# Deformable convolutions and a mixture of experts on one core: another order of the pixels in a tile's partitions

## The chip, the cores and the metric

The kernel runs on one core of a Trainium2 chip. The metric is the device time of one launch in microseconds. The core has five instruction streams that run beside each other and meet at semaphores: PE (matrix products and transposes), DVE (vector work), ACT (activations, scaled copies), POOL (here it only issues indirect DMAs) and SP (issues the plain DMAs). Sixteen DMA engines move the data of both issuers.

## The reference, cut to what matters

The input x has 4 images of 256 channels and 64 x 64 pixels. After a normalisation over channels, three modulated deformable 3 x 3 convolutions follow, each with a ReLU, then a residual sum, a layer norm over channels, and a mixture of 8 experts (the best two for each pixel).

```python
def _deform_layer(x, w_off, b_off, w, b):
    om = conv3x3(x, w_off) + b_off                 # 27 channels
    off = om[:, :2 * K].reshape(B, K, 2, H, W)     # K = 9 taps
    mask = jax.nn.sigmoid(om[:, 2 * K:])
    ys = gy + base_y + off[:, :, 0]
    xs = gx + base_x + off[:, :, 1]
    sampled = _bilinear(x, ys, xs) * mask[:, None] # [B, C, K, H, W]
    return einsum('bikhw,oik->bohw', sampled, wk) + b

for wo, bo, w, b in params:                        # three layers
    x = relu(_deform_layer(x, wo, bo, w, b))
```

For every pixel and tap, four neighbouring pixels with all their 256 channels are blended, at a place that depends on the data.

## The kernel before, in words

An image is cut into 8 blocks (NB) of 512 pixels (BLK, 8 image rows), and a block into 4 tiles (TPB) of 128 pixels, two image rows each. In a tile, partition p holds pixel p % 64 of row p // 64. The twelve pairs of layer and image are run as stages in the order of `self.stages` (L860): (0,0), (1,0), (0,1), (2,0), (1,1), (0,2), (2,1), (1,2), (0,3), (2,2), (1,3), (2,3), with the layer first. For each block of a stage `main_block` runs; beside it, in small steps (`step`, `aside`), the preparation of the next layer's blocks, and from a queue with credits (`pump`) the experts' work of images that are through.

The source of the samples is a table in DRAM for each image and layer (`store_table`): one row of 2048 bytes per pixel, with its 256 channels and their differences to the image row below. Two table rows that follow each other are two pixels side by side, so 4096 bytes hold all that one bilinear sample needs.

The plan of a block is made in `off_block`. PE computes the offset convolution into the PSUM tile `po`, in four strips of 32 partitions; ACT copies it with the bias to `om` [128, 512], pixels along the free axis in raster order (L337). Then for each tile t a matmul with `om[:, t*128:(t+1)*128]` as its stationary operand turns it (L342), so that pixel t*128+p arrives in partition p of `pm`. DVE adds `base` (the host's table of each partition's pixel coordinates, L921 to L925), takes floors and fractions, and stores the indices `idx` and the coefficients `cf`.

`main_block` runs over the 9 taps k and the 4 tiles. For each pair POOL issues one indirect DMA (L452) that fetches for each of the 128 partitions the 4096 bytes at the table row in `idx`, into one of 10 buffers `g`. DVE blends in one direction (L458), ACT scales the left half (L463), DVE adds the right half (L468), giving `s` with pixels in partitions; PE transposes it (L472) and ACT copies the result to `sT` (L477), channels in partitions and pixels along the free axis. PE multiplies `sT` with the tap's weights into `acc` (L480), which holds both halves of the output channels for the 512 pixels in one PSUM buffer, across all taps.

At the end of a block `acc` is evicted: ACT takes the first half of the channels (L500), DVE the second (L501), both with bias and ReLU. For layers 0 and 1 the target is the window `w` of the next layer (10 rows of 66 pixels with a border), for layer 2 it is the tile `r` for the tokens. What follows (`rows_done`, `store_table`, `off_block`, or `tokens`) reads pixels in raster order.

The order of the program is that of the loops and generators. The order in which instructions stand on an engine is made from it at compile time; the timeline shows L458 and L468 in other orders than the loop's.

Of the kernel before, what the change touches and what calls it, by code (L numbers as in the profile page):

```python
# [10 lines left out]
AF = mybir.ActivationFunctionType  # L11
ALU = mybir.AluOpType
# [9 lines left out]
CC = C // P  # L22
# [4 lines left out]
NB = H * W // BLK  # L27
RPB = BLK // W
J = TPB * K

# [52 lines left out]
class Weave:  # L85
# [231 lines left out]
    def off_block(self, l, b, n, w):  # L317

        nc = self.nc
        nm = f"{l}_{b}_{n}"  # L320


        po = self.ps1.tile([P, BLK], F32, tag="po", name=f"po_{nm}")
        terms = [(k, c) for k in range(K) for c in range(CC)]
        for m, (k, c) in enumerate(terms):
            ky, kx = divmod(k, 3)
            g = m % NQ
            nc.tensor.matmul(  # L328
                po[g * Q : (g + 1) * Q, :],
                lhsT=self.wo[l][:, k, c, :],  # L330
                rhs=w[:, c, ky : ky + RPB, kx : kx + W],
                start=(m < NQ),
                stop=(m + NQ >= len(terms)),
                tile_position=(0, g * Q),
            )
        om = self.small.tile([P, BLK], F32, tag="om", name=f"om_{nm}")
        nc.scalar.activation(om, po, AF.Identity, bias=self.bo[l])  # L337
        yield
        pm = self.ps.tile([P, TPB, 3 * K], F32, tag="tp", name=f"pm_{nm}")
        for t in range(TPB):  # L340

            nc.tensor.matmul(  # L342
                pm[:, t, :],
                lhsT=om[:, t * P : (t + 1) * P],
                rhs=self.strips[:, : 3 * K],
                start=True,
                stop=True,
            )

        def small(tag, shape=(P, 2, J), dt=F32):  # L350
            return self.small.tile(list(shape), dt, tag=tag, name=f"{tag}_{nm}")

        idx = self.plan.tile([P, J], I32, tag="idx", name=f"idx_{nm}")
        cf = self.plan.tile([P, J, 3], F32, tag="cf", name=f"cf_{nm}")
        self.plans[l, b, n] = (idx, cf)

        th = small("th", (P, J))
        nc.scalar.activation(
            th.rearrange("p (t k) -> p t k", k=K), pm[:, :, 2 * K :], AF.Tanh, scale=0.5
        )  # L360
        pos = small("pos")
        for d in range(2):
            nc.vector.tensor_tensor(
                pos[:, d, :].rearrange("p (t k) -> p t k", k=K),
                pm[:, :, d : 2 * K : 2],
                self.base[:, n, d, :, :],
                ALU.add,
            )

        nc.vector.tensor_scalar(pos, pos, -1.0, float(H), ALU.max, ALU.min)  # L370
        pi = small("pi", dt=I32)
        nc.vector.tensor_copy(pi, pos)
        yield
        pf = small("pf")
        nc.vector.tensor_copy(pf, pi)
        up = small("up")
        nc.vector.tensor_tensor(up, pf, pos, ALU.is_gt)
        fl = small("fl")
        nc.vector.tensor_tensor(fl, pf, up, ALU.subtract)
        fr = small("fr")  # L380
        nc.vector.tensor_tensor(fr, pos, fl, ALU.subtract)
        ixf = small("ixf", (P, J))
        nc.vector.scalar_tensor_tensor(
            ixf, fl[:, 0, :], float(TC), fl[:, 1, :], ALU.mult, ALU.add
        )
        nc.vector.tensor_scalar(idx, ixf, float(TC + 1), None, ALU.add)
        yield

        nc.vector.tensor_copy(cf[:, :, 0], fr[:, 0, :])
        for q, (s0, s1) in enumerate(((-0.5, 0.5), (0.5, 0.0))):  # L390
            hf = small(f"hf{q}", (P, J))
            nc.vector.tensor_scalar(hf, fr[:, 1, :], s0, s1, ALU.mult, ALU.add)
            nc.vector.scalar_tensor_tensor(cf[:, :, 1 + q], th, 1.0, hf, ALU.add, ALU.mult)
# [43 lines left out]
    def main_block(self, i, n, wins):  # L437
        nc = self.nc
        l, b = self.stages[i]
        nm = f"{i}_{n}"  # L440
        idx, cf = self.plans.pop((l, b, n))
        tb = self.table(l, b)
        acc = self.ps1.tile([P, CC, BLK], F32, tag="acc", name=f"acc_{nm}")
        for k in range(K):
            sT = self.smT.tile([P, CC, BLK], F32, tag="sT", name=f"sT_{nm}_{k}")
            for t0 in range(0, TPB, 2):
                tp = self.ps.tile([P, CC, 2 * P], F32, tag="tp", name=f"tp_{nm}_{k}_{t0}")
                gs, ss = [], []
                for t in (t0, t0 + 1):
                    j = t * K + k  # L450
                    g = self.gat.tile([P, 2, 2, C], F32, tag="g", name=f"g_{nm}_{j}")
                    nc.gpsimd.indirect_dma_start(  # L452
                        out=g.rearrange("p x s f -> p (x s f)"),
                        out_offset=None,
                        in_=tb,
                        in_offset=bass.IndirectOffsetOnAxis(ap=idx[:, j : j + 1], axis=0),
                    )
                    nc.vector.scalar_tensor_tensor(  # L458
                        g[:, :, 0, :], g[:, :, 1, :], cf[:, j, 0:1], g[:, :, 0, :],
                        ALU.mult, ALU.add,  # L460
                    )
                    s = self.smp.tile([P, C], F32, tag="s", name=f"s_{nm}_{j}")
                    nc.scalar.activation(s, g[:, 0, 0, :], AF.Copy, scale=cf[:, j, 1:2])  # L463
                    gs.append(g)
                    ss.append(s)
                for u in range(2):
                    j = (t0 + u) * K + k
                    nc.vector.scalar_tensor_tensor(  # L468
                        ss[u], gs[u][:, 1, 0, :], cf[:, j, 2:3], ss[u], ALU.mult, ALU.add
                    )  # L470
                    for c in range(CC):
                        nc.tensor.transpose(  # L472
                            tp[:, c, u * P : (u + 1) * P],
                            ss[u][:, c * P : (c + 1) * P],
                            self.ident,
                        )
                nc.scalar.copy(sT[:, :, t0 * P : (t0 + 2) * P], tp)  # L477
            for o in range(CC):
                for c in range(CC):
                    nc.tensor.matmul(  # L480
                        acc[:, o, :],
                        lhsT=self.wk[k][:, c, o * P : (o + 1) * P],
                        rhs=sT[:, c, :],
                        start=(k == 0 and c == 0),
                        stop=(k == K - 1 and c == CC - 1),
                    )
            if n == NB - 1 and i + 1 < len(self.stages):
                self.load_tap(self.stages[i + 1][0], k, i + 1)
            self.step(k)
            self.pump()  # L490
        bk = self.bk[l]
        if l < NL - 1:
            w = wins[n] = self.window(n, nm, False)
            dst = [w[:, o, 1 : RPB + 1, 1 : W + 1] for o in range(CC)]
            src = [acc[:, o, :].rearrange("p (r w) -> p r w", w=W) for o in range(CC)]
        else:
            r = self.big.tile([P, CC, BLK], F32, tag="a", name=f"r_{nm}")
            dst = [r[:, o, :] for o in range(CC)]
            src = [acc[:, o, :] for o in range(CC)]
        nc.scalar.activation(dst[0], src[0], AF.Relu, bias=bk[:, 0:1])  # L500
        nc.vector.tensor_scalar(dst[1], src[1], bk[:, 1:2], 0.0, ALU.add, ALU.max)  # L501
        if l < NL - 1:
            self.rows_done(l + 1, b, n, wins)
        else:
            self.aside(5, self.tokens(b, n, r))
# [432 lines left out]
```

## Time and profile before

Eleven runs give a median of 8170.06 us, from 8149.62 to 8199.07. The profiled execution took 8176.97 us, and its span from the first to the last instruction is 8175.3 us.

| engine | busy, us | share | instructions |
|---|---|---|---|
| PE | 6704.9 | 82% | 27032 |
| DVE | 4918.7 | 60% | 10768 |
| ACT | 3566.5 | 44% | 7368 |
| POOL | 4476.3 | 55% | 4133 |

The granted TensorE clock is 0.926 on average. The DMA engines moved 2314 MB in 744,472 packets, 283 GB/s over the span. The costliest groups by line:

| line, engine | what | count | busy, us | mean, ns |
|---|---|---|---|---|
| L452 POOL | issue of a gather | 3456 | 3766.6 | 1090 |
| L480 PE | product with the tap's weights | 6912 | 3409.1 | 638 |
| L458 DVE | first blend, 128 x 512 | 3456 | 2528.3 | 744 |
| L463 ACT | scaling, 128 x 256 | 3456 | 1673.6 | 511 |
| L468 DVE | second blend, 128 x 256 | 3456 | 1617.3 | 481 |

In a line of the waits, the engine and line on the left stood idle until the one on the right was done; the numbers are the total in us, how often, and the longest. In a line of the timeline stand the start in us, the duration in us, the engine, the line, the operation, and in brackets the idle time before it with what ended it. In a line for one source line stand the shortest, the median and the longest duration in ns. Busy times of engines overlap, so they don't add up to the span.

### The profile page before, as it was taken

Reading aid. Unit: us, or ns where it says so; the run is one execution under the profiler, and the core shown is the slowest. Engines: PE = TensorE matmul, PEld = TensorE weight load, DVE = VectorE, ACT = ScalarE, POOL = GpSimd, SP = SyncE. Lnnn points to the kernel's source line nnn. Section 1 sums busy time; section 2 is a strip of 40 time slices with the busy share of each in tenths; the row PEclk is TensorE's granted clock in tenths of the full one; section 3 lists DMA queues with packets and bytes.
Section 4 is the critical chain, followed back from the end, with each engine's and each line's share of the span. In section 5 each row is a group of like instructions: output and inputs, shape, how many; then the busy total and the mean of one; then the engine's idle time right before and its main releaser. Section 6 shows DMA issues by size and latency. Waiting matters only on the chain. (4 is left out here: it accounts for less than half of the span.)

```text
span 8175.3 us, 91172 instructions
## 1 busy us (share of the span) xinstructions
PE 6704.9 (82%) x27032; PEld 3751.3 (46%) x27032; DVE 4918.7 (60%) x10768; ACT 3566.5 (44%) x7368; POOL 4476.3 (55%) x4133
## 2 busy tenths in 40 slices
PE   5898888888876999998866799998866889896395
PEld 2444444444442555555433455555532455563274
DVE  4776677777774666667665566666754555565201
ACT  3454444445442444545443444545433443443121
POOL 0554666665556566655566565665666544456413
PEclk8999999999997999999988999999978999997697
DMA  5987899998887898988787889898887777787433
GB/s 172 365 305 269 320 324 321 328 329 312 290 289 242 313 326 320 324 318 297 255 302 258 284 312 333 325 332 316 290 286 250 265 271 262 283 286 257 151 124 119
DMA packets 744472, 2314.47 MB, mean 283 GB/s; under 512 B 104344, under 2 KB 148376, under 8 KB 735784
## 3 DMA queue, kind: packets, MB, share of 16 engines
q0 software_dynamic: 544704, 1954.99, 67.2%
q1 hardware_dynamic: 199272, 353.64, 12.2%
q8 instruction: 217, 3.56, 0.2%
q14 instruction: 279, 2.29, 0.1%
HBM read 2167.35 MB, written 249.61 MB: 296 GB/s over the span
## 5 line engine op out<-in xcount | busy, mean ns | idle before, releaser
L452 POOL DMA_INDIRECT g<-tab,idx x3456 | 3766.6, 1090 | 2687.8 <-DVE s L468 1305.9
L480 PE MATMUL acc<-sT,wk 128*128 128x512 f32 x6912 | 3409.1, 638 | 356.6 <-ACT sT L477 232.7
L458 DVE SCALAR_TENSOR_TENSOR g<-g,cf 128x512 f32<-128x512 f32 x3456 | 2528.3, 744 | 478.9 <-DMA g<-tab,idx 383.6
L468 DVE SCALAR_TENSOR_TENSOR s<-g,cf,s 128x256 f32<-128x256 f32 x3456 | 1617.3, 481 | 1601.4 <-ACT s L463 1260.5
L463 ACT ACTIVATE s<-g,cf 128x256 f32<-128x256 f32 x3456 | 1673.6, 511 | 1674.6 <-DVE g L458 1107.8
L480 PEld LDWEIGHTS acc<-sT,wk 128*128 128x128 f32 x6912 | 1332.1, 202 | 2049.4 <-issue 1521.5
L472 PE MATMUL tp<-ident,s 128*128 128x128 f32 x6912 | 1082.0, 283 | 462.0 <-DVE s L468 327.0
L477 ACT COPY sT<-tp 128x512 f32<-128x512 f32 x1728 | 970.7, 587 | 1011.3 <-PE tp L472 688.3
L472 PEld LDWEIGHTS tp<-ident,s 128*128 128x128 f32 x6912 | 823.5, 145 | 947.4 <-issue 499.8
L765 PE MATMUL py<-w,hT 128*128 128x256 f32 x2496 | 637.3, 392 | 69.2 <-ACT hT L760 50.0
L750 PE MATMUL ph<-fzT,w 128*128 128x256 f32 x2496 | 620.0, 392 | 22.0 <-issue 7.8
L750 PEld LDWEIGHTS ph<-fzT,w 128*128 128x128 f32 x2496 | 479.8, 195 | 168.5 <-issue 55.2
L765 PEld LDWEIGHTS py<-w,hT 128*128 128x128 f32 x2496 | 458.5, 192 | 210.1 <-ACT hT L760 107.3
L706 POOL DMA_INDIRECT w<-in_W,wrow x156 | 177.2, 1136 | 653.4 <-issue 307.5
L760 ACT ACTIVATE hT<-ph,w 128x256 f32<-128x256 f32 x624 | 261.3, 470 | 533.4 <-PE ph L750 345.0
L328 PE MATMUL po<-win,wo 128*32 128x512 f32 x2304 | 455.9, 616 | 46.5 <-ACT win L263 35.0
L773 DVE TENSOR_TENSOR y<-py,w 128x512 f32<-128x512 f32 x156 | 107.5, 689 | 461.1 <-PE py L765 457.1
L794 POOL DMA_INDIRECT gy<-ys,slots x256 | 264.2, 1032 | 211.1 <-DVE ta L802 88.7
L681 POOL DMA_INDIRECT zs<-zl,slots x256 | 267.1, 1043 | 136.1 <-issue 70.7
L298 ACT COPY hv<-tpv 128x512 f32<-128x512 f32 x384 | 214.4, 595 | 227.1 <-PE tpv L293 117.0
L328 PE MATMUL po<-win_pre,wo 128*32 128x512 f32 x1152 | 229.7, 644 | 22.7 <-ACT win_pre L422 7.6
L293 PE MATMUL tpv<-ident,vv 128*128 128x128 f32 x768 | 156.8, 285 | 26.4 <-ACT sT L477 17.1
(144 smaller groups left out, 3237.3 us busy)
## 6 DMA issues: line engine op xcount, KB each, us to landing
tab<-hv SPq DMA_DIRECT2D x384, 256.0 KB
g<-tab,idx POOLq DMA_INDIRECT x3456
zt<-zs SPq DMA_DIRECT2D x156, 256.0 KB
ys<-y SPq DMA_DIRECT2D x156, 256.0 KB
wk<-in_conv_w SPq DMA_DIRECT2D x108, 256.0 KB
zs<-nil SPq DMA_DIRECT2D x38, 512.0 KB
xc_pre<-in_x SPq DMA_DIRECT2D x32, 512.0 KB
xr_tok<-in_x SPq DMA_DIRECT2D x32, 512.0 KB
```

Of the source, the lines that this page charges most:

```text
L328: nc.tensor.matmul(po[g * Q : (g + 1) * Q, :], lhsT=self.wo[l][:, k, c, :], rhs=w[:, c, ky : ky + RPB, kx : kx + W], start=(m < NQ), stop= ...
L452: nc.gpsimd.indirect_dma_start(out=g.rearrange("p x s f -> p (x s f)"), out_offset=None, in_=tb, in_offset=bass.IndirectOffsetOnAxis(ap=id ...
L458: nc.vector.scalar_tensor_tensor(g[:, :, 0, :], g[:, :, 1, :], cf[:, j, 0:1], g[:, :, 0, :], ALU.mult, ALU.add,)
L463: nc.scalar.activation(s, g[:, 0, 0, :], AF.Copy, scale=cf[:, j, 1:2])
L468: nc.vector.scalar_tensor_tensor(ss[u], gs[u][:, 1, 0, :], cf[:, j, 2:3], ss[u], ALU.mult, ALU.add)
L472: nc.tensor.transpose(tp[:, c, u * P : (u + 1) * P], ss[u][:, c * P : (c + 1) * P], self.ident,)
L477: nc.scalar.copy(sT[:, :, t0 * P : (t0 + 2) * P], tp)
L480: nc.tensor.matmul(acc[:, o, :], lhsT=self.wk[k][:, c, o * P : (o + 1) * P], rhs=sT[:, c, :], start=(k == 0 and c == 0), stop=(k == K - 1 ...
L681: ins = self.nc.gpsimd.indirect_dma_start(out=self.zs[grp.i % 2], out_offset=bass.IndirectOffsetOnAxis(ap=grp.slots[:, i, m : m + 1], axis=0),
L750: nc.tensor.matmul(ph[:, h, :], lhsT=w1[:, o : o + P], rhs=zT[:, c, :], start=(c == 0), stop=(c == CC - 1),)
L765: nc.tensor.matmul(py[:, u, :], lhsT=hT[h // 2][:, h % 2, u * P : (u + 1) * P], rhs=w2[:, h * C : (h + 1) * C], start=(h == 0), stop=(h == ...
L794: nc.gpsimd.indirect_dma_start(out=g, out_offset=None, in_=self.ys[grp.i % 2], in_offset=bass.IndirectOffsetOnAxis(ap=grp.slots[:, i, m : ...
```

## The change

The order of the 64 pixels of an image row in the 64 partitions of a half tile is changed. Each half row of 32 pixels was laid into 32 partitions in raster order. Now partition 4e + j of such a group holds pixel 8j + e, with e from 0 to 7 and j from 0 to 3. Partitions that lie four apart hold neighbouring pixels; partitions side by side hold pixels that lie 8 apart.

The permutation enters where ACT copies `po` to `om` (the written address jumps by 4 elements for neighbouring pixels), and the host's `base` names the new coordinates. Indices, coefficients, gathers, blends, transposes and products follow in the new order with no other change. It is undone at the eviction: `acc` is read in its own order and written to raster positions, so neighbouring elements are written 8 elements (32 bytes) apart. The pattern has too many dimensions for one instruction, so each of the two becomes one per half row (h).

```diff
-        nc.scalar.activation(om, po, AF.Identity, bias=self.bo[l])
+        nc.scalar.activation(
+            om.rearrange("p (q e j) -> p q j e", e=8, j=4),
+            po.rearrange("p (q j e) -> p q j e", e=8, j=4),
+            AF.Identity,
+            bias=self.bo[l],
+        )
...
             w = wins[n] = self.window(n, nm, False)
-            dst = [w[:, o, 1 : RPB + 1, 1 : W + 1] for o in range(CC)]
-            src = [acc[:, o, :].rearrange("p (r w) -> p r w", w=W) for o in range(CC)]
+            dst = w[:, :, 1 : RPB + 1, 1 : W + 1]
         else:
             r = self.big.tile([P, CC, BLK], F32, tag="a", name=f"r_{nm}")
-            dst = [r[:, o, :] for o in range(CC)]
-            src = [acc[:, o, :] for o in range(CC)]
-        nc.scalar.activation(dst[0], src[0], AF.Relu, bias=bk[:, 0:1])
-        nc.vector.tensor_scalar(dst[1], src[1], bk[:, 1:2], 0.0, ALU.add, ALU.max)
+            dst = r.rearrange("p c (r w) -> p c r w", w=W)
+        dst = dst.rearrange("p c r (h j e) -> p c h r e j", j=4, e=8)
+        src = acc.rearrange("p c (r h e j) -> p c h r e j", h=2, e=8, j=4)
+        for h in range(2):
+            nc.scalar.activation(dst[:, 0, h], src[:, 0, h], AF.Relu, bias=bk[:, 0:1])
+            nc.vector.tensor_scalar(
+                dst[:, 1, h], src[:, 1, h], bk[:, 1:2], 0.0, ALU.add, ALU.max
+            )
...
-    base[:, :, 1] = p % W + k % 3 - 1 + 0 * (n + t)
+    base[:, :, 1] = p // 32 % 2 * 32 + p % 4 * 8 + p % 32 // 4 + k % 3 - 1 + 0 * (n + t)
```

## The prediction

> **What bounds the kernel now.** I read the page's head first, then the groups of instructions by cost, the waits by total, a stretch of the timeline in the steady part, and last the rows of the lines that the diff touches. The page's chain of waits covers only the last part, where the FFN of the fourth image runs alone (PE with 2% is its largest share), so it says nothing of the stages in which the gathers run; those are read from the waits.
>
> ```profile
> DMA  5987899998887898988787889898887777787433
> q0 software_dynamic: 544704, 1954.99, 67.2%
> q1 hardware_dynamic: 199272, 353.64, 12.2%
> ```
>
> The 16 DMA engines are busy 8 to 9 tenths where the convolutions run, and most of that is q0, which carries the gathers. That looks like a DMA bound. The waits say that it is not:
>
> ```profile
> POOL g L452 <- DVE s L468: 1305.9, 1100, 10.4
> DVE s L468 <- ACT s L463: 1260.5, 1220, 20.1
> ACT s L463 <- DVE g L458: 1107.8, 1048, 12.0
> DVE g L458 <- DMA g<-tab,idx: 383.6, 284, 11.6
> ```
>
> The instruction that consumes a gather, L458, waited for the gather's landing 284 times out of 3456, 383.6 us in all. The issuer waits more than three times as long for a free buffer. The timeline shows why:
>
> ```profile
> 1004.11 0.75 DVE L458 SCALAR_TENSOR_TENSOR g<-g,cf 128x512 f32<-128x512 f32 x1
> ...
> 1004.47 1.20 POOL L452 DMA_INDIRECT g<-tab,idx  x1 [1.08 <-DVE s L468]
> ...
> 1004.90 0.51 ACT L463 ACTIVATE s<-g,cf 128x256 f32<-128x256 f32 x1 [1.22 <-DVE g L458]
> ...
> 1005.44 0.48 DVE L468 SCALAR_TENSOR_TENSOR s<-g,cf,s 128x256 f32<-128x256 f32 x1 [0.58 <-ACT s L463]
> ...
> 1005.84 0.74 DVE L458 SCALAR_TENSOR_TENSOR g<-g,cf 128x512 f32<-128x512 f32 x1
> ...
> 1006.19 1.20 POOL L452 DMA_INDIRECT g<-tab,idx  x1 [0.52 <-DVE s L468]
> ```
>
> One sample tile costs 0.75 + 0.51 + 0.48 us in series over DVE, ACT, DVE, and the next L458 starts 1.73 us after the first without waiting for data. Setting the packets of q0 in order of issue against the starts of L458, I find a median of 8.4 us between the moment when a gather's 128 packets are through and its use; 79% have over 4 us, 11% under 1.5 us. Those late ones lie in stages (2,0), (2,1), (1,3) and (2,3), where the next indices come late and POOL issues just in time. So faster fetching can pay only in about 300 gathers, while slower fetching pays nothing until the slack is used up.
>
> **The change, part by part.**
>
> *Order of the rows in a gather.* Nothing is added on POOL or in bytes. What it can alter is how long packets take. The packet records of q0 have 458,752 packets of 4096 bytes with a median of 159 ns and a mean of 183 ns: 82% stand at the floor, 7.9% take over 200 ns and bear nearly all of the excess. An engine moves 8 packets per gather, so stalled ones (about 10 of 128) make the slowest of the 16 engines some 0.9 us late (8 x 24 ns mean, plus two or three hits of some 300 ns on the unluckiest). No run here has the new order, so I bound: all stalls gone, 300 late gathers x 0.9 us = -270 us; excess doubled, two hits more on the unluckiest, 300 x 0.6 = +180 us, and the densest stages (DMA share 0.91) reach 0.91 + 8 x 24 ns / 1.74 us = 1.02, which on (1,0) and (0,1), 1000 us, adds 20 more: +200 us. The nearest row is the spread between stages: offsets differ much by layer (their standard deviation, from the reference's inputs, is 0.48, 0.15 and 0.08 pixels), yet the share of stalled packets moves only between 5.8% and 9.5%. So I let it move by one point of eight, downward because more common rows are read at a time: 270 / 8 = 34, taken as **-30 us**.
>
> *The eviction of acc.* One ACT and one DVE instruction of 512 elements become two each of 256, 96 times.
>
> ```profile
> L500 ACT ACTIVATE win<-acc,bk x64: 670/689/692, 267.9 to 6874.2; 128x512 f32<-128x512 f32 x64
> L501 DVE TENSOR_SCALAR win<-acc,bk x64: 739/752/754, 268.6 to 6874.9; 128x512 f32<-128x512 f32 x64
>   PE acc L480: 148.5, 73
>   DVE win L501: 64.4, 29
>   ACT r L500: 32.4, 12
> L651 DVE TENSOR_REDUCE sf<-r x8: 568/586/594, 2433.0 to 7645.6; 128x32 f32<-128x256 f32 x8
> L662 DVE TENSOR_REDUCE ex<-r x4: 465/466/477, 2431.8 to 7643.1; 128x39 f32<-128x312 f32 x4
> ```
>
> DVE starts 0.7 us after ACT, at ACT's end, though they read and write different halves. I take it that the four new instructions are chained likewise, ACT, DVE, ACT, DVE. Of 256 elements from PSUM, L760 on ACT takes 468 ns and L68 on DVE 536, so some 500 each: 4 x 0.50 + 3 x 0.034 = 2.10 us against 0.69 + 0.034 + 0.75 = 1.47, **+0.63 us**. The elements are now written 32 bytes apart. The one row like it is L651, which reads 256 elements 128 bytes apart in 586 ns; L662 reads 312 in a row in 466, so 256 would take about 408, and the stride costs 178 ns. Below, 0; above, 4 x 0.178 = 0.71 us: the eviction grows by 0.63 to 1.35 us, taken 0.9, nearer the lower end because a read is not a write. If the halves were not chained, 2 x 0.5 = 1.0 us would stand against 1.47, a gain of 0.45 us: the bound below. What waits: ACT's second half waits for DVE, and behind it in ACT's queue stand the copies L477 and the scalings L463 of the next block, behind those PE's matmuls. How often this counts: in 73 of 96 blocks ACT stood idle for the last matmul of acc, in 41 (29 + 12) DVE stood idle for ACT. Between 0.43 and 0.76 I take 0.6: 96 x 0.9 x 0.6 = **+52 us**, bounds 96 x 0.45 x 0.6 = -26 and 96 x 1.35 x 0.76 = +98.
>
> *The copy om (L337).* Still one instruction, 687 ns, written 16 bytes apart: 0 to 2 x 178 = 356 ns, x 96 = 0 to 34 us. PE waited for it in 52 of 96 blocks; half of half: **+10 us**.
>
> *base* is only other numbers in the same 288 KB load: nothing.
>
> Against the Trainium skill, for those who have it: SBUF — State Buffer (section Door 1: The DMA port swizzle) says that each access in a new line of 16 bytes pays. L651 agrees for reads (586 against about 408 ns); no row shows a write. By that rule both stores pay fully, and the sum would be 8177 + 78 + 34 - 30 = 8259 instead of the 8209 below. DMA: Bandwidth & Descriptors (section The descriptor swizzle) gives each engine four partitions in a row, so that the engines now fetch pixels four apart, 8 KB, at a time, and then neighbours. With that map and the sample positions, stalls in the present records are fewer in gathers where more engines read near the same row at once; drawn out to the new order, an estimate with a wide error, about half would go: 8177 + 62 - 135 = 8104.
>
> **Sum.** Against the profiled execution, 8176.97 us (span 8175.3 and 1.7 around it): 8177 - 30 + 52 + 10 = 8209. The median of the eleven runs is 7 us lower, so 8202, said as **8205 us**.
>
> **The rivals.**
>
> *Faster: the fetch gains more than the eviction costs.* Neighbours at a time halve the stalls: 300 x 0.45 = -135, and the eviction has no stride cost, 96 x 0.63 x 0.6 = +36: 8170 - 99 = about 8070 us. It decides from the point where the fetch gives back 62 us, a quarter of 270: stalled packets falling from 7.9% to under 6%. For it: the 24 ns of excess stand mostly in stretches with gathers alone, so gathers disturb gathers. Against it: 8.4 us of slack, and only 284 waits.
>
> *Much slower: the fetch becomes the bound.* If engines that read the same rows queue behind one another and the excess triples (72 ns, 231 per packet), the share of the dense stages (1,0), (0,1), (0,2), (0,3), 2170 us, becomes 0.91 + 8 x 48 / 1740 = 1.13: +280 us, late gathers 300 x 1.2 = +360, the two stores +62: about 8870; doubled only, 8170 + 200 + 62 = 8432. For it: DMA at 0.9. Against it: the spread by layer is small.
>
> *It does nothing for fetching and the eviction is hidden,* for ACT is busy 44% and DVE 60%: 8170. Against it: 41 blocks in which DVE waited for ACT.
>
> Below all of these lies the order in which the instructions stand on each engine: in the trace L458 and L468 alternate singly in some blocks and in pairs in others, so that order is not the loop's, and it can shift when instructions are added. I have no price for that but some +-40 us, half a per cent.
>
> **How the numbers follow.** Forecast 0.40 (8180 to 8270), faster by the fetch 0.33, nothing 0.14, fetch as the bound 0.13. About 0.2%, 16 us, is what a measurement of this kernel can tell from no change. The forecast and the last case lie above it: slower 0.53; same 0.14; faster 0.33. The range goes from 8030 (the faster case and 40 us) to 8340 (the excess up by half, 8170 + 100 + 62, rounded up), leaving about one in ten at each side.
>
> **What would show it.** L500 and L501 with 192 each; about 0.5 us each if strides are free, near 0.68 if not, in turn ACT, DVE, ACT, DVE. L337 at 687 or towards 1040 ns. The share of q0 and the wait of L458 for its gather: 67.2% and 383.6 us falling together mean the rival on the faster side, rising together the one on the slower. If the wait falls and the time does not, the path is where I say. The forecast is wrong if the wait of L458 falls by more than 100 us, or if DVE no longer waits for ACT.

## The result, and the profile after

The changed kernel takes 8258.11 us, the median of 8 runs (8238.43 to 8271.76); beside it the kernel before took 8175.35. The ratio is 1.010, with a 95% interval of 1.0084 to 1.0117: slower by 1%, some 83 us. The forecast was 8205 us, slower, in a range of 8030 to 8340.

The head of the page after, the DMA engines and their queues, is to be held against the three lines of before in the prediction:

```profile
DMA  4997888898887898888787888888887777787433
q0 software_dynamic: 544704, 1954.99, 66.8%
q1 hardware_dynamic: 199272, 353.64, 12.2%
```

The same packets, the same bytes, and almost the same share (67.2% before, of a span 1% shorter). The packet records say it more sharply. Of the 458,752 packets of 4096 bytes on q0, the mean was 182.9 ns and is 183.5; the median was 159 and is 159; over 200 ns were 8.08% and are 8.08%. The new order left no mark on the fetch.

The waits after, with the waiting engine and line, what ended the wait, total us, times and the longest:

```profile
POOL g L459 <- DVE s L475: 1397.3, 1068, 10.3
...
DVE g L465 <- DMA g<-tab,idx: 367.9, 282, 8.8
...
DVE win L509 <- ACT win L508: 107.3, 63, 10.1
```

L465 (L458 before) waits for its gather 282 times where it was 284, 367.9 us where it was 383.6. What has grown is the eviction. The rows of its lines and of om (shortest, median and longest duration in ns):

```profile
L508 ACT ACTIVATE win<-acc,bk x128: 674/696/738, 275.0 to 6957.0; 128x256 f32<-128x256 f32 x128
L509 DVE TENSOR_SCALAR win<-acc,bk x128: 637/652/685, 275.7 to 6957.8; 128x256 f32<-128x256 f32 x128
L508 ACT ACTIVATE r<-acc,bk x64: 643/696/757, 1883.3 to 7698.7; 128x256 f32<-128x256 f32 x64
L509 DVE TENSOR_SCALAR r<-acc,bk x64: 637/654/679, 1884.0 to 7699.4; 128x256 f32<-128x256 f32 x64
L339 ACT ACTIVATE om<-po,bo x96: 1147/1180/1234, 48.3 to 6970.7; 128x512 f32<-128x512 f32 x96
```

ACT needs 696 ns for half as many elements as before took 688: twice the instructions, each as long. The copy to om went from 687 to 1180 ns. One eviction in the timeline of the changed kernel, ACT first and DVE below (start and duration in us):

```profile
848.72 0.70 ACT L508 ACTIVATE win<-acc,bk 128x256 f32<-128x256 f32 x1 [1.27 <-issue]
...
850.14 0.69 ACT L508 ACTIVATE win<-acc,bk 128x256 f32<-128x256 f32 x1
```

```profile
849.45 0.66 DVE L509 TENSOR_SCALAR win<-acc,bk 128x256 f32<-128x256 f32 x1 [0.81 <-issue]
...
850.87 0.65 DVE L509 TENSOR_SCALAR win<-acc,bk 128x256 f32<-128x256 f32 x1 [0.19 <-ACT win L508]
```

ACT, DVE, ACT, DVE, each 0.03 to 0.04 us after the end of the one before: 2.80 us from 848.72 to 851.52. Over all 96 evictions the median went from 1.48 to 2.90 us and the mean from 1.60 to 3.47. The loss builds up with the stages: between the two profiles their first gathers start 25 us later in (2,0), 41 us in (0,3) and 83 us in (2,3); the experts' work at the end adds nothing.

### The profile page after: what moved, and what is told of

Same layout as the page of the kernel before. It is cut to its first block, busy times and chain, and to the rows that moved or that the text cites. A ratio compares the mean times of both kernels' runs of the same rounds, so it can differ in the third digit from the quotient of the medians.

```text
span 8251.3 us, 91352 instructions
## 1 busy us (share of the span) xinstructions
PE 6737.2 (82%) x27032; PEld 3763.7 (46%) x27032; DVE 4956.5 (60%) x10864; ACT 3648.3 (44%) x7466; POOL 4413.9 (53%) x4133
## 5 line engine op out<-in xcount | busy, mean ns | idle before, releaser
L459 POOL DMA_INDIRECT g<-tab,idx x3456 | 3703.0, 1071 | 2833.3 <-DVE s L475 1397.3
L465 DVE SCALAR_TENSOR_TENSOR g<-g,cf 128x512 f32<-128x512 f32 x3456 | 2525.1, 744 | 455.9 <-DMA g<-tab,idx 367.9
L470 ACT ACTIVATE s<-g,cf 128x256 f32<-128x256 f32 x3456 | 1668.3, 510 | 1696.7 <-DVE g L465 1076.6
L749 PE MATMUL ftp<-ident,zt 128*128 128x128 f32 x624 | 98.3, 279 | 98.0 <-DMA zt<-zs 93.9
```

What stands on the lines that cost most here:

```text
L459: nc.gpsimd.indirect_dma_start(out=g.rearrange("p x s f -> p (x s f)"), out_offset=None, in_=tb, in_offset=bass.IndirectOffsetOnAxis(ap=id ...
L465: nc.vector.scalar_tensor_tensor(g[:, :, 0, :], g[:, :, 1, :], cf[:, j, 0:1], g[:, :, 0, :], ALU.mult, ALU.add,)
```

## The experiments

Twelve kernels ran, in four groups: e1 to e4, e5 to e8, u1 with u2 and e9, and e10. Beside them the kernel before took 7751, 7759, 8185 and 7759 us, so times of different groups are not compared; ratios are, each against the kernel before of its own group, with a 95% interval in brackets.

**The fetch order alone** (e1), with every instruction in the place it has in the kernel before:

```diff
-    base[:, :, 1] = p % W + k % 3 - 1 + 0 * (n + t)
+    base[:, :, 1] = p // 32 % 2 * 32 + p % 4 * 8 + p % 32 // 4 + k % 3 - 1 + 0 * (n + t)
```

> The kernel before with the new base alone: every instruction, and the order on each engine, is that of before; only the addresses that the gathers fetch follow the new order (the offsets then belong to other pixels, and the output is in another order). Theory (the fetch is indifferent to the order): 4096-byte packets at 183 ns mean and 8.1% over 200 ns as before, time within 0.2% of before. Rival (the neighbours do speed the fetch, and the stores of the change cost more than it brings): mean under 178 ns, time at least 0.4% under before. Rival (neighbours slow it): mean over 188 ns and time over before.

Ratio 1.0009 (1.0000 to 1.0018). Packets 181.9 ns at the mean, 6.9% over 200; e4 below, on the same chip with the old order, has 181.9 and 7.1%. The order does nothing for the fetch.

**The stores alone** (e2): the changed kernel with the old `base`, the same diff the other way round.

> The changed kernel with the old base: all instructions of the change, gathers in raster order (offsets of other pixels, output in another order). Theory (all of the loss is the stores of om and acc and what they shift): ratio to before 1.010, within 0.002 of the changed kernel. Rival (part of the loss is the fetch): ratio under 1.006. Rival (the fetch gains and hides part): ratio over 1.014.

Ratio 1.0107 (1.0088 to 1.0126), the whole loss. With e1 this settles where it comes from: the two copies and the order of instructions that goes with them, not the addresses.

**The eviction alone** (e3), om and base as before, and **the copy to om alone** (e4):

```diff
-        nc.scalar.activation(dst[0], src[0], AF.Relu, bias=bk[:, 0:1])
-        nc.vector.tensor_scalar(dst[1], src[1], bk[:, 1:2], 0.0, ALU.add, ALU.max)
+        dst = dst.rearrange("p c r (h j e) -> p c h r e j", j=4, e=8)
+        src = acc.rearrange("p c (r h e j) -> p c h r e j", h=2, e=8, j=4)
+        for h in range(2):
...
```

> The kernel before with the change's eviction of acc alone (om and base as before; output pixels in another order). The eviction took 3.47 us on average after the change against 1.60 before, 96 times 1.86 us = 179 us at the most. Theory (the eviction bears most): ratio 1.006 to 1.010. Rival (the copy to om bears it, 96 times 0.49 us = 47 us): ratio under 1.003. Rival (it is the shifted order of instructions): no fixed value, and the parts do not add up to the whole.

```diff
-        nc.scalar.activation(om, po, AF.Identity, bias=self.bo[l])
+        nc.scalar.activation(
+            om.rearrange("p (q e j) -> p q j e", e=8, j=4),
+            po.rearrange("p (q j e) -> p q j e", e=8, j=4),
...
```

> The kernel before with the change's copy to om alone (1180 ns in place of 687; eviction and base as before; the offsets belong to other pixels). Theory: beside other work, ratio 1.000 to 1.003. Rival (the copy bears the loss): ratio up to 1.006, which is 47 us.

The eviction: 1.0097 (1.0083 to 1.0110). The copy: 1.0033 (1.0021 to 1.0045), which is 26 us of the 47 that 96 copies of 0.49 us more amount to; 1.000 to 1.003 was expected, and it came a little above. The two add up to 1.30% where the whole is 1.07%; the intervals of the three are wide enough for that, so whether the parts overlap is not shown. In e4 the order on PE, DVE and POOL is that of the kernel before, and on ACT the same but for the copies' own rows. Since other addresses with other pixels' offsets cost at most 0.18% in e1, its 26 us go to the longer copy, though that share is not shown by itself.

**Splitting without the stride** (e5): half rows in raster order.

```diff
+        dst = dst.rearrange("p c r (h e) -> p c h r e", h=2)
+        src = acc.rearrange("p c (r h e) -> p c h r e", h=2, e=32)
+        for h in range(2):
...
```

> The kernel before with its eviction split in two half rows per half of the channels, pixels in raster order, no stride (four instructions in place of two; the output is the reference's). Theory (the stride is what costs: 696 and 652 ns for 256 elements, as long as 512 in a row): instructions of about 470 on ACT and 490 on DVE, a chain of 2.0 us, ratio 1.001 to 1.004, less than half of the whole eviction's 1.0097. Rival (the splitting costs, by its longer chain): ratio 1.006 and over.

**The stride without splitting** (e6): one instruction of 512 for each half of the channels.

```diff
+        dst = dst.rearrange("p c r (j e) -> p c r e j", j=8, e=8)
+        src = acc.rearrange("p c (r e j) -> p c r e j", e=8, j=8)
+        nc.scalar.activation(dst[:, 0], src[:, 0], AF.Relu, bias=bk[:, 0:1])
...
```

> The kernel before with its two eviction instructions unsplit, 512 elements each, written 32 bytes apart (8 x 8 transposed in each image row, so output pixels in another order). Theory (stride alone): about 1180 ns on ACT as the copy to om, some 1100 on DVE, a chain of 2.3 us, ratio 1.003 to 1.007. Rival (splitting): 690 and 750 ns and ratio under 1.002.

The rows of the eviction in e5, and then in e6:

```profile
L501 ACT ACTIVATE win<-acc,bk x128: 462/481/518, 268.9 to 6538.5; 128x256 f32<-128x256 f32 x128
L502 DVE TENSOR_SCALAR win<-acc,bk x128: 471/485/488, 269.4 to 6539.0; 128x256 f32<-128x256 f32 x128
```

```profile
L500 ACT ACTIVATE win<-acc,bk x64: 1167/1177/1212, 271.2 to 6563.8; 128x512 f32<-128x512 f32 x64
L501 DVE TENSOR_SCALAR win<-acc,bk x64: 1125/1130/1172, 272.4 to 6565.1; 128x512 f32<-128x512 f32 x64
```

The price of the stride is plain: 256 elements 481 to 696 ns on ACT and 485 to 652 on DVE, 512 elements 689 to 1177 and 752 to 1130. That is 0.7 to 1.0 ns for each element. The ratios are 1.0018 (1.0008 to 1.0028) for e5 and 1.0045 (1.0031 to 1.0059) for e6. Most of the eviction's 0.97% is the stride; the split, with the order that it shifts, costs 0.18%. On every engine e5 has the order of e3 (on DVE and ACT up to 3% of the rows differ, the eviction's own), while e6 has the order of the kernel before, so its 0.45% comes from the longer instructions without a new order.

**The other end of the range for the fetch**: samples anywhere in the image (e7), and all samples of a tile at one pixel but for the offsets (e8).

```diff
+    rng = np.random.RandomState(1)
+    base[:, :, 0] = rng.randint(0, H, (P, NB, TPB, K))
+    base[:, :, 1] = rng.randint(0, W, (P, NB, TPB, K))
```

> The kernel before with a base of random pixels of the image, so that the samples fetched at a time lie anywhere in the 9 MB table (samples and output are of other pixels); all instructions as before. Theory (packets do not care where samples lie): 4096-byte packets at 182 ns mean, ratio 0.998 to 1.002. Rival (neighbourhood matters, and both orders compared so far are near): mean over 190 ns and a slower kernel.

```diff
+    base[:, :, 0] = RPB * n + 2 * t + 0 * (p + k)
+    base[:, :, 1] = W // 2 + 0 * (p + n + t + k)
```

> The kernel before with a base that names one pixel per tile for all partitions, so that all 16 engines read the same few table rows (samples and output are of other pixels); all instructions as before. Theory: packets at 182 ns, ratio 0.998 to 1.002. Rival (engines on the same rows stand in each other's way): mean over 200 ns, slower. Rival (the same rows are faster): mean under 170 ns; the time then falls little, by at most the 627 us for which DVE and POOL wait for gathers in the kernel before on this chip, more likely 100.

The share of q0 and the wait of L458 for its gather, of e7 and then of e8:

```profile
q0 software_dynamic: 544704, 1954.99, 70.6%
...
DVE g L458 <- DMA g<-tab,idx: 541.1, 423, 9.8
```

```profile
q0 software_dynamic: 544704, 1954.99, 70.2%
...
DVE g L458 <- DMA g<-tab,idx: 611.4, 463, 9.1
```

Packets: 182.1 ns and 7.0% over 200 scattered, 181.9 ns and 7.9% on one pixel. On the same chip e5 and e6, both in raster order, have 181.7 and 182.2 ns at the mean and 7.1 and 7.2% over 200, so neither extreme moves the mean by more than two kernels of one order differ. The share over 200 is higher on one pixel, and counting the packets that start between the first gathers of two stages shows where: in (2,0), (2,1), (2,2) and (2,3), the stages of layer 2, it is 10.1, 10.8, 8.6 and 10.3% against 8.8, 8.3, 6.9 and 7.7% in e5. The scattered kernel has the spread of e5 (3.9 to 8.8% over the stages, and 3.8 to 8.8). e7 takes 0.9994 (0.9985 to 1.0004) of the time. e8 takes 1.0058 (1.0043 to 1.0073), which the theory did not allow; its mean packet doesn't show why. Between the profiles of e1 and e8, 8 of 32 us have come up by the first gather of the last stage, 17 come up in that stage and 7 in the experts' work at the end, whose rows are written and read by data. The last stage is one of those with more stalled packets; whether they are the cause was not tried, and it stays open.

**The chain taken away.** In the kernel before DVE's eviction waits for ACT's although they touch different halves. With `acc` as two PSUM tiles it waits for PE instead; u1 does this to the kernel before, u2 to the changed one.

```diff
-        acc = self.ps1.tile([P, CC, BLK], F32, tag="acc", name=f"acc_{nm}")
+        acc = [
+            self.ps1.tile([P, BLK], F32, tag=f"acc{o}", name=f"acc{o}_{nm}") for o in range(CC)
+        ]
```

> The kernel before with the two halves of acc as two PSUM tiles of one bank each, all else as before (output is the reference's). DVE's eviction then waits for PE, not for ACT. Theory (the chain over ACT and DVE is on the path, about half of each microsecond of it counts): 0.7 us less on each of 96 evictions, 69 us, ratio 0.994 to 0.998. Rival (the chain is covered, and only busy time of ACT and DVE counts): ratio 0.999 to 1.001. The order on PE changes too, which can blur it.

> The changed kernel with the two halves of acc as two PSUM tiles: the same four strided instructions of 0.70 and 0.65 us, but ACT's and DVE's beside each other, 1.4 us in place of 2.8. Theory (chain on the path): 132 us less of chain, about half of it counts, ratio to before 1.001 to 1.006. Rival (the busy time alone counts): 1.009 to 1.011 as the change.

u1: 0.9996 (0.9977 to 1.0016). From PE's last product to the end of the eviction it takes 0.79 us at the median in place of 1.51, and nothing is gained that can be told: the 0.7 us of chain that went had cost little or nothing. u2: 1.0050 (1.0033 to 1.0066), half of the loss, with instructions about as long as the change's (689 and 644 ns) and 1.32 us to the end in place of 2.94. So the theory was wrong for the kernel before, and its range held for the changed one. (The order on PE shifts in both, on about a fifth of its rows in u1, so some tenths of a per cent may be that.)

**The stride on the reading side** (e9): the change with its inner loops turned round, so that PSUM is read with the stride and SBUF is written in a row.

```diff
-        dst = dst.rearrange("p c r (h j e) -> p c h r e j", j=4, e=8)
-        src = acc.rearrange("p c (r h e j) -> p c h r e j", h=2, e=8, j=4)
+        dst = dst.rearrange("p c r (h j e) -> p c h r j e", j=4, e=8)
+        src = acc.rearrange("p c (r h e j) -> p c h r j e", h=2, e=8, j=4)
```

> The changed kernel with the inner loops of om and of the eviction turned round: ACT and DVE write in a row and read PSUM with the stride (16 bytes in acc, 32 in po), same results as the change. Theory (what costs is the stride on the written side, in SBUF): om 690 ns, halves of 480 and 490, ratio 1.001 to 1.003 as with the split in raster order. Rival (a stride on either side costs the same): om 1180, halves 700 and 650, ratio 1.010.

```profile
L508 ACT ACTIVATE win<-acc,bk x128: 461/481/518, 272.5 to 6917.7; 128x256 f32<-128x256 f32 x128
L509 DVE TENSOR_SCALAR win<-acc,bk x128: 471/485/487, 273.0 to 6918.2; 128x256 f32<-128x256 f32 x128
...
L339 ACT ACTIVATE om<-po,bo x96: 672/687/712, 49.1 to 6930.5; 128x512 f32<-128x512 f32 x96
```

481, 485 and 687 ns, the medians without any stride, to the nanosecond (481 and 485 in e5, 687 in the kernel before). The ratio is 1.0039 (1.0022 to 1.0057), above the 1.001 to 1.003 that were expected, and over half of the loss is gone by turning two loops. On every engine e9 has the order of the changed kernel, so only the durations differ between the two. What is left is the split and its order; in raster order on another chip (e5) these cost 1.0018, with an interval that overlaps this one.

**What could a faster fetch bring?** (e10) One table row for each sample in place of two:

```diff
-                        out=g.rearrange("p x s f -> p (x s f)"),
+                        out=g[:, 0].rearrange("p s f -> p (s f)"),
...
-                        g[:, :, 0, :], g[:, :, 1, :], cf[:, j, 0:1], g[:, :, 0, :],
-                        ALU.mult, ALU.add,
+                        g[:, :, 0, :], g[:, 0:1, 1, :].to_broadcast([P, 2, C]), cf[:, j, 0:1],
+                        self.half, ALU.mult, ALU.add,
```

> The kernel before with half of each gather: one table row of 2048 bytes per partition in place of two (the right pixel's half is not fetched, and the first blend takes it from the left one's and a constant; same counts and sizes of instructions on DVE, ACT and PE; their order on the engines shifts, for the compiler reckons with shorter transfers). It asks what any faster fetch could bring. Theory (the fetch is hidden but for the late gathers): the packets of q0 take about 84 ns in place of 159, its share falls from 67% to under 40%, and the time falls by what L458 and POOL wait for gathers at the most, 440 us on one chip and 627 on the other, more likely by 50 to 200: ratio 0.975 to 0.995. Rival (DMA at 9 tenths is the bound of the dense stages): ratio 0.90 or less. Rival (nothing at all): 0.998 to 1.002.

No theory held: 1.102 (1.0998 to 1.1041), ten per cent slower with half of the bytes. DMA engines, q0, the first blend with the idle time before it, and its wait:

```profile
DMA  5654555555555555555465555555556555555433
...
q0 software_dynamic: 323520, 1049.02, 41.4%
...
L460 DVE SCALAR_TENSOR_TENSOR g<-g,cf,half 128x512 f32<-128x512 f32 x3456 | 2550.3, 749 | 2558.0 <-DMA g<-tab,idx 2544.1
...
DVE g L460 <- DMA g<-tab,idx: 2544.1, 2047, 17.7
```

The same wait in e1:

```profile
DVE g L458 <- DMA g<-tab,idx: 554.6, 421, 10.4
```

The DMA engines are busy only 5 tenths, and DVE waits 2544 us for gathers where it waited 555 in e1. The packets are not those that were expected, either. Instead of 2048-byte packets of 84 ns the records of q0 have about half as many of 4096 bytes (237,568) as before; their median stays at 159 ns, the mean rises to 221, and 22% take over 200 ns. Every engine's order differs from that of the kernel before: there a first blend stands alone between second blends 1494 times, here 333 times. The likely cause, argued and not tried by itself, is that order: reckoning with short transfers, the compiler put first blends close behind their gathers. In a stretch of its timeline five second blends (L470) stand behind one first blend, and then DVE is idle for 2.56 us until the next gather lands:

```profile
1000.03 2.06 DVE L470 SCALAR_TENSOR_TENSOR s<-g,cf,s 128x256 f32<-128x256 f32 x5
1004.65 0.75 DVE L460 SCALAR_TENSOR_TENSOR g<-g,cf,half 128x512 f32<-128x512 f32 x1 [2.56 <-DMA g<-tab,idx]
```

By this account the blended buffers wait for their second blend and are not free for new gathers, and the latency of a gather shows, although it is shorter than in e1 (3.7 us from issue to landing at the median, and 6.5). So this kernel does not answer the question that it was made for; that stays open. It shows that the slack of the kernel before can be lost while the DMA engines have less to do.

No kernel here beats the kernel before; u1 and e7 equal it within their intervals.

## Why the prediction came out

The direction, the place of the loss (the eviction) and its chain of four steps came out. The size did not: the three terms sum to 32 us, and 83 were measured. The fetch gave back nothing where 30 us were forecast, the eviction alone cost 75 us in place of 52, and the copy om 26 in place of 10.

**The bound.** That DMA, busy 8 to 9 tenths, was not what the dense stages waited for, was read from the waits and from the 8.4 us between landing and use, and nothing speaks against it. But the experiments with addresses left the mean packet as it was, so they could not test it, and e10 shows only that the slack can be lost. What does bound each stage is not shown. Two stretches of the kernel before, the first in (1,0) and (0,1), the second almost all in (0,2) (start and end, length, the busy us of PE, its weight loads, DVE, ACT and POOL with the counts in brackets, the granted clock, the DMA share, GB/s):

```profile
1100.00:1600.00 500.00, 428.33 (x1635) 203.55 (x1634) 357.05 (x730) 243.37 (x504) 309.29 (x289) 0.98 0.91 324
3100.00:3600.00 500.00, 481.79 (x1985) 276.96 (x1984) 333.03 (x657) 248.14 (x527) 314.61 (x276) 0.99 0.90 326
```

In the second PE itself is busy 482 of 500 us. The prediction weighs the blends on DVE and ACT against DMA, and PE's load not at all; that PE bounds such a stage is a rival that no run here tests.

**The fetch, -30 us, bounds -270 to +200.** Measured: e1 is 0.09% slower, 7 us, with an interval that reaches down to 0. The direction of this term was a guess from the spread between stages; that spread is not one of neighbourhood, for scattering the samples leaves it as it was, and piling them up raises the share in layer 2, against the guess. The rule drawn on beside it (the Trainium skill, DMA: Bandwidth & Descriptors, section The descriptor swizzle) says which partitions an engine serves; no run shows that, and it does not matter here. The estimate made with it, half of the stalled packets gone, was wrong: 8.08% before (the prediction has 7.9) and after. The correlation behind it did not survive a run that changed the addresses alone.

**The eviction, +52 us.** The chain in four steps was right, and with the growth of the plain case (2.80 against 1.47) the factor of 0.6 comes out: 96 x 1.33 us x 0.6 = 77 us, and e3 shows 0.97% of 7751, 75 us. That is luck in part. By the mean growth over all evictions, 1.86 us, the factor would be 0.4, and in e5, where the eviction ends 0.98 us later at the median, 14 us are 0.15 of that growth. What was off is the price of the stride: the growth was taken at 0.9 us in all, 0.27 of it for the stride, nearer the lower end "because a read is not a write"; it came at 1.33, close to the upper bound of 1.35. The rule of the Trainium skill (SBUF — State Buffer, section Door 1: The DMA port swizzle) that each access in a new line of 16 bytes pays, agrees with the writes here (215 ns more for 256 elements on ACT, 167 on DVE), and the sum that went by it, 8259 us, was nearest to the measured time. That nearness is luck in part too, for the sum has the -30 us of the fetch, which did not come, and 78 and 34 us for the two copies, which cost 75 and 26 alone. Reading PSUM at strides of 16 and 32 bytes paid nothing (e9).

The reason given for the factor, blocks in which DVE stood idle for ACT, was not sound: u1 takes that wait away and gains nothing that can be told. Set side by side, with the loss as (ratio - 1) times the time of the kernel before in the same group, and the busy time added as count times the difference of the durations:

| kernel | added on ACT + DVE, us | eviction's end after PE's last product, median, us | loss, us |
|---|---|---|---|
| before | 0 | 1.51 | 0 |
| u1, two tiles | 0 | 0.79 | -3 |
| e4, om | 47 + 0 | 1.51 | 26 |
| e5, split | 26 + 21 | 2.49 | 14 |
| e9, read side | 26 + 21 | 2.49 | 32 |
| e6, stride | 48 + 37 | 2.39 | 35 |
| u2, change with two tiles | 112 + 51 | 1.32 | 41 |
| e3, eviction | 68 + 54 | 2.94 | 75 |
| the change | 115 + 54 | 2.94 | 83 |

The length of the chain alone does not order the losses (e5 and e6 end alike), and neither does the busy time alone (u2 and the change). Added busy time costs 0.3 to 0.7 of itself where the chain stands, and a quarter of itself in u2, where it does not. The prediction counted the chain; it should have counted what ACT and DVE have more to do as well. How the two share the loss is not settled, nor what the order of instructions adds: only e4 and e6 have that of the kernel before, and the losses have intervals of some 8 to 16 us to each side.

**The copy om, +10 us, bounds 0 to 34.** It grew by 493 ns, over the bound of 356 that was taken from the one strided read, and cost 26 us. The count behind the factor was doubled: the 52 waits are 26 of PE's weight loads and 26 of its products, at the same moments, so PE waited for the copy in 26 blocks of 96 and not in 52. With that count the term would have been 5 us, still further off.

**The rivals.** The faster one fell with the fetch. The fetch as the bound did not come. That the eviction is hidden was right for the 0.7 of its 1.5 us that u1 takes away, and wrong for 2.9. The +-40 us for a shifted order held for the change (e5, 0.18% with the split), and e10 suggests that it is no bound in general.

## What to carry to other kernels

When a permutation is folded into a copy from PSUM to SBUF, let the loop run so that the stride is on PSUM's side and the write goes in a row: here that made the difference between 1180 and 687 ns for the same 512 elements. Before an order of addresses is optimised, change the addresses alone, with every instruction in its place, and try the extremes; three kernels told that the mean packet of 4096 bytes from this table takes the same time wherever the rows lie. And a wait seen in the profile prices nothing until the work behind it is found: taking 0.7 us off each eviction had no effect that could be told, adding 1.3 had.

## What was not expected of the hardware

- The excess of the gathers' packets over 159 ns, 22 to 24 ns at the mean from 7 to 8% of packets, does not depend on where the samples lie: raster, neighbours, random places and one single place gave 181.7 to 182.7 ns in e1 to e8. Only the share over 200 ns rose in layer 2 when all samples of a tile lay at one place (8.6 to 10.8% by stage). With half of each row pair (e10) the mean was 221 ns. What stalls them stays open.
- For a write stride in SBUF (16 or 32 bytes on ACT, 32 on DVE) ACT paid 0.8 to 1.0 ns for each element and DVE 0.7, about as much as for the element itself (0.8 and 1.0 ns, from 256 against 512 elements). For reading PSUM at such a stride they paid nothing.
- The same kernel took 7751 to 7759 us beside three groups of experiments and 8185 beside another. The granted clock was 0.94 in its runs of the former and 0.92 in those of the latter, a smaller difference than the 5% in time. The record gives the number 1 to the chip of the group at 8185 and to that of one at 7759, so the number does not tell them apart.
